# Perceiver stream: where GpSimd's key subtractions and the context loads stand, and how the short last key chunks are grouped

## Chip, cores and metric

The kernel runs on one core of a Trainium2 chip. Its time is the device time of one execution in microseconds (us), as the median of three runs. TensorE (PE), VectorE (DVE), ScalarE (ACT), GpSimd (POOL) and SyncE (SP) each run their own instructions in program order. Here all DMAs are issued from SyncE's queue, which is in order too.

## What is computed

Two perceiver layers on 32 batches of 64 queries of width 256. Only the two cross attentions touch the large input, a context of 1601 keys per batch:

```python
x = x + _L0_xattn_ref(_layernorm(x), ctx_1024, ctx_1024, wq, bq, wk, bk, wv, bv, wo, bo)
x = x + _L0_attn_ref(_layernorm(x), ...)        # self attention
x = x + _L0_ffn_ref(_layernorm(x), ...)         # attention over the best half of the tokens
x = x + _L1_xattn_ref(_layernorm(x), ctx_1024, mask, q_w, q_b, k_w, k_b, v_w, v_b)
x = x + _L1_attn_ref(...); x = x + _L1_ffn_ref(...)
# a cross attention, 16 heads of 16:
scores = softmax(einsum('bhqd,bhkd->bhqk', qh, kh)); attn = einsum('bhqk,bhkd->bhqd', scores, vh)
```

## The kernel before, in words

The method `stream` does both cross attentions and, between them in time, the first layer's self attention and feed-forward. It counts 64 batches: 32 of the first layer, then the same 32 of the second. What follows it (the second layer's self attention and feed-forward, from about 3400 us on) is not touched.

**Units.** A unit `u` is one batch and 4 of its 16 heads: 256 units, each of 4 iterations `i`. In an iteration TensorE gets, in this order: score products `sp` for the next unit's row maxima (`maxima`, L1093; 3, 3, 2 and 0 groups in iterations 0 to 3, VectorE reduces each, L1098; three PSUM buffers), the value products `acc` of the iteration before (`weighted`, L1145), score products `tp` for the exponentials (`probabilities`, L1128, evacuated by ScalarE as `e`, L1133), a step of the other attentions (`group_step`), and key and value products (`keys_values`).

**Keys and values.** The 1601 keys of a batch are 13 chunks of 128; the last holds 65 keys, or 72 with padding. A key group is two chunks, `KEYGROUPS`: six full groups and a seventh with the short chunk alone. A group goes through these steps, written as generators:

- `load` (L892): a DMA of the context into `raw`, three buffers.
- `split`: VectorE rounds `raw` to `chi` (L904), GpSimd subtracts, `clo` (L905).
- `keys`: 12 f32r matmuls into the bank `kp` (L980), ScalarE adds the bias, `kr` (L986).
- `parted`: VectorE casts `kr` to bf16 (L936), GpSimd subtracts (`kr`, L937), VectorE casts the rest, GpSimd subtracts again (`ks`, L937), and SyncE stores the three parts to DRAM, `kd` (L942). Each `yield` of it ends a step; `tick` runs one step of each open group.
- `values`: 12 matmuls, or 6 for the short chunk, into the bank `vp` (L1006); ScalarE copies them to `v` (L1011).

`projections` puts these in order: a load four groups ahead just before `keys(i)`, the split two groups ahead just before `values(i)`. `keys_values` runs banks until the work made, in the planner's column counts (`PER_BATCH`), meets a target that lies 1.8 batches ahead of the unit.

**Fetches.** At a unit's start `fetch` calls `tick` and then issues the seven DMAs (L1065, L1069) that bring the keys of the unit after next from `kd` into `kst`, three buffers; the buffer comes free with the last `tp` of the unit before. `tick` is called again in each iteration just ahead of `probabilities`, so there are five ticks in a unit. In the tick, the cast and the subtraction behind it stand together:

```python
                    nc.vector.tensor_copy(ks[:, s, :, :m], x)
                    eng.tensor_tensor(
                        x if s == 0 else ks[:, 2, :, :m], x, ks[:, s, :, :m], ALU.subtract
                    )
                    if s or not quick:
                        yield
```

Of the kernel before, what the change touches and what calls it, by code (L numbers as in the profile page):

```python
# [19 lines left out]
F32 = mybir.dt.float32  # L20
# [9 lines left out]
P = 128  # L30
# [7 lines left out]
NKE = 1608  # L38
KEYGROUPS = [(c, min(2, NCH - c)) for c in range(0, NCH, 2)]
GB = len(KEYGROUPS)  # L40
KG = 2 * P
NATGROUPS = [(0, 401), (401, 400), (801, 400), (1201, 400)]
# [17 lines left out]
class Kernel:  # L60
# [411 lines left out]
    def stream(self):  # L472
        nc, tc, ins = self.nc, self.tc, self.ins
        with ExitStack() as ctx:
# [13 lines left out]
            dkv = pool("dk", 3, space=DRAM)  # L488
# [399 lines left out]
            def load(b, g, raw=None):  # L888
                c0, n = KEYGROUPS[g]
                if raw is None:  # L890
                    raw = inp.tile([P, 2, KG], F32, tag="raw", name=f"raw{b}_{g}", bufs=3)
                nc.sync.dma_start(  # L892
                    raw[:, :, : n * P],
                    ins["ctx_1024"][b % NB, :, c0 * P : (c0 + n) * P].rearrange(
                        "(c p) n -> p c n", p=P
                    ),
                )
                return raw

            def split(b, g, raw):  # L900
                n = KEYGROUPS[g][1] * P
                hi = inp.tile([P, 2, KG], F32R, tag="chi", name=f"chi{b}_{g}", bufs=3)
                lo = inp.tile([P, 2, KG], F32R, tag="clo", name=f"clo{b}_{g}", bufs=3)
                nc.vector.tensor_copy(hi[:, :, :n], raw[:, :, :n])  # L904
                (nc.vector if b == 0 and g < 2 else nc.gpsimd).tensor_tensor(  # L905
                    lo[:, :, :n], raw[:, :, :n], hi[:, :, :n].bitcast(F32), ALU.subtract
                )
                return hi, lo

            kds, vs, ksts, cuts = {}, {}, {}, []  # L910

            vring = []
            for g, (_, n) in enumerate(KEYGROUPS):
                vring.append([
                    vp_.tile([P, n, 16, 17], F32, tag=f"v{g}_{r}", name=f"v{g}_{r}")
                    for r in range(3 if g < 5 else 2)
                ])
                for v in vring[g]:
                    nc.gpsimd.memset(v[:, :, :, 16:17], 1.0)

            def tick(b=-1):

                for one in list(cuts):
                    while next(one[1], True) is None:
                        if one[0] > b:
                            break
                    else:
                        cuts.remove(one)

            def parted(b, g, k0, m, r, quick):  # L930

                ks = work.tile([P, 3, 2, KG], BF16, tag="ks", name=f"ks{b}_{g}")
                eng = nc.vector if quick else nc.gpsimd
                x = r[:, :, :m]
                for s in range(2):
                    nc.vector.tensor_copy(ks[:, s, :, :m], x)  # L936
                    eng.tensor_tensor(  # L937
                        x if s == 0 else ks[:, 2, :, :m], x, ks[:, s, :, :m], ALU.subtract
                    )
                    if s or not quick:  # L940
                        yield
                nc.sync.dma_start(  # L942
                    kds[b][:, :, k0 : k0 + m].rearrange("s (c p) n -> p s c n", p=P),
                    ks[:, :, :, :m],
                )

            seq = [(b, g) for b in range(2 * NB) for g in range(len(KEYGROUPS))]

# [9 lines left out]
            keyed, valued = [0], [0]  # L958

            def projections():  # L960


                parts = {0: split(*seq[0], raws.pop(0))}
                wk, wv = cut(wraw.pop(), 0, 1), None
                turn = NB * GB

                def keys(i):
                    b, g = seq[i]
                    c0, n = KEYGROUPS[g]
                    m = min(n * P, NKE - c0 * P)  # L970
                    hi, lo = parts[i]
                    if g == 0:
                        kds[b] = dkv.tile([3, D, NKP], BF16, tag="kd", name=f"kd{b}")
                    r = work.tile([P, 2, KG], F32, tag="kr", name=f"kr{b}_{g}")
                    kp = bank(f"kp{b}_{g}").rearrange("p (c n) -> p c n", c=2)
                    for oc in range(2):
                        j = 0
                        for w, x in ((0, hi), (1, hi), (0, lo)):
                            for cc in range(2):
                                nc.tensor.matmul(  # L980
                                    kp[:, oc, :m], wk[w][:, cc, oc * P : (oc + 1) * P],
                                    x[:, cc, :m], start=(j == 0), stop=(j == 5),
                                )
                                j += 1
                    for oc in range(2):
                        nc.scalar.activation(  # L986
                            r[:, oc, :m], kp[:, oc, :m], AF.Identity,
                            bias=self.bk[layer(b)][:, oc : oc + 1],
                        )
                    cuts.append((b, parted(b, g, c0 * P, m, r, i < 10)))  # L990
                    keyed[0] = i + 1
                    return 12 * max(m, P)

                def values(i):
                    b, g = seq[i]
                    n = KEYGROUPS[g][1]
                    hi, lo = parts.pop(i)
                    v = vring[g][b % len(vring[g])]
                    vs.setdefault(b, []).extend(v[:, i0] for i0 in range(n))
                    vp = bank(f"vp{b}_{g}").rearrange("p (i d) -> p i d", i=2)  # L1000
                    for i1 in range(n):
                        o = slice(i1 * P, (i1 + 1) * P)
                        j = 0
                        for cc in range(2):
                            for x, w in ((hi, 0), (hi, 1), (lo, 0)):
                                nc.tensor.matmul(  # L1006
                                    vp[:, i1, :], x[:, cc, o], wv[w][:, cc, :],
                                    start=(j == 0), stop=(j == 5),
                                )
                                j += 1  # L1010
                    nc.scalar.copy(  # L1011
                        v[:, :, :, :16],
                        vp[:, :n, :].rearrange("p c (h d) -> p c h d", d=16),
                    )
                    valued[0] = i + 1
                    return 6 * n * D

                def fetched(i):
                    if i < len(seq) and i not in raws and i not in parts:
                        raws[i] = load(*seq[i])  # L1020

                parts[1] = split(*seq[1], raws.pop(1))
                two = []
                for i in range(len(seq)):
                    if i == turn - 2:
                        two.append(weight(1, 1))
                    elif i == turn - 1:
                        two.append(weight(1, 2))
                    elif i > 4 and i != turn:
                        fetched(i + 4)  # L1030
                    yield keys(i)
                    if i + 2 < len(seq):
                        parts[i + 2] = split(*seq[i + 2], raws.pop(i + 2))
# [4 lines left out]
                    if i == turn - 1:  # L1038
                        wk = cut(two[0], 1, 1)
                        fetched(i + 3)  # L1040
                        fetched(i + 4)
                    if i == turn:
                        wv = cut(two[1], 1, 2)
                        fetched(i + 4)
                    yield values(i)

            PER_BATCH = sum(
                12 * max(min(n * P, NKE - c0 * P), P) + 6 * D * n for c0, n in KEYGROUPS
            )
# [6 lines left out]
            def fetch(u):  # L1056

                b, q4 = divmod(u, 4)
                while keyed[0] < (b + 1) * GB:
                    made[0] += next(proj)  # L1060
                tick(b)
# [74 lines left out]
            def weighted(u, i, e):  # L1136
# [3 lines left out]
                v = vs[b]  # L1140
                assert valued[0] > b * GB + i
                for c in range(2 * i, min(2 * i + 2, NCH)):
                    m = min(P, NK - c * P)
                    for h in range(4):
                        nc.tensor.matmul(  # L1145
                            acc[32 * h : 32 * h + 17, slot, :], v[c][:m, 4 * q4 + h, :],
# [52 lines left out]
            raws = {0: load(*seq[0])}  # L1199
            wraw = [weight(0, 1)]  # L1200
            self.bk = self.biases(wp, 0, "k")
            raws[1] = load(*seq[1])
# [5 lines left out]
            raws[2] = load(*seq[2])  # L1208
            early = kp_.tile([P, 4, NKE], BF16, tag="kst", name="early")
            early = early.rearrange("p h n -> p (h n)").bitcast(F32)  # L1210
            for i in range(5):
                raws[3 + i] = load(
                    *seq[3 + i],
# [9 lines left out]
            def banks_made(n):  # L1223
                for _ in range(n):
                    made[0] += next(proj)
                    tick()
# [4 lines left out]
            while keyed[0] < GB:  # L1231
# [16 lines left out]
            for u in range(NU):  # L1248
# [11 lines left out]
                for i in range(4):  # L1260
# [10 lines left out]
                    tick()  # L1271
# [5 lines left out]
                    keys_values(LEAD + (4 * u + i + 1) / 16.0, 0.15)  # L1277
                    end_step()
# [925 lines left out]
```

## Time and profile before

| | |
|---|---|
| three runs | 3994.56 us median (3990.45 to 4006.71) |
| the profiled execution | 3997.09 us, of which its span 3995.4 |
| instructions | 155308 |
| DMA | 647 MB, 162 GB/s over the span |
| `kd<-ks` stores | 384 of 384 KB, 64 of 108 KB |
| `raw` loads | 380 of 256 KB, 63 of 128 KB |
| `kst<-kd` fetches | 1536 of 201 KB |

A page's group line names line, engine and operation, the tile written and those read, partitions x elements and type, and the count; then busy time in us and the mean in ns of one; then the engine's idle time just before, and who ended it. Two groups of each engine that the change touches:

```profile
L937 POOL TENSOR_TENSOR kr<-kr,ks 128x512 f32<-128x512 f32 x438 | 487.5, 1113 | 1148.3 <-DVE ks L936 1083.8
L936 DVE CAST ks<-kr 128x512 bf16<-128x512 f32 (+1 forms) x896 | 537.5, 600 | 527.3 <-ACT kr L986 279.7
...
L905 POOL TENSOR_TENSOR clo<-raw,chi 128x512 fp32r<-128x512 f32 x441 | 541.3, 1227 | 78.5 <-issue 16.8
```

The first line reads: 438 subtractions of 1113 ns; GpSimd was idle for 1148 us before them, 1084 of these until VectorE's cast was done. Rows that keep shapes apart give the 128x512 casts (768) 608 ns, the 128x144 casts (128) 551, `chi` casts of 128x512 (380) 505, and the short group's evacuations by ScalarE 318.

### The profile page before, as it was taken

The numbers are of one execution on the slowest core, as the hardware profiler recorded it, in microseconds if no ns is written. First come the engines' busy times: TensorE is split into PE (matmuls) and PEld (weight loads), VectorE is DVE, ScalarE is ACT, GpSimd is POOL, SyncE is SP. The second block draws the span as 40 slices with busy tenths as digits, with TensorE's granted clock in tenths as the row PEclk, the third lists the DMA queues.
The fourth block names the chain that finished last, engine by engine and source line by source line (L and its number), as shares of the span: only waits on it lengthen the run. The fifth ranks groups of instructions, "written<-read, shape, count | busy, mean of one in ns | idle before, by whom it ended". The sixth has DMA issues, their size and how long they took to land.

```text
span 3995.4 us, 155308 instructions
## 1 busy us (share of the span) xinstructions
PE 3594.5 (90%) x66703; PEld 2893.7 (72%) x66703; DVE 2785.4 (70%) x6723; ACT 2016.5 (50%) x4015; POOL 2007.6 (50%) x2234
## 2 busy tenths in 40 slices
PE   6899999999999998999999999998999998674589
PEld 6788878778788887777777777777777776331467
DVE  5567767666767766667776766666766665688879
ACT  2455555555555554455555555554555554142453
POOL 3455555555555555555655556555555552004246
PEclk8999999999999999999999999999999999785689
DMA  6888768767777776767777777667787786100000
GB/s 171 217 210 205 196 160 203 190 175 193 187 188 196 191 183 174 198 171 190 178 185 183 183 188 193 176 166 187 196 205 197 198 202 165 55 1 1 1 4 20
DMA packets 669952, 647.05 MB, mean 162 GB/s; under 512 B 98064, under 2 KB 567376, under 8 KB 669136
## 3 DMA queue, kind: packets, MB, share of 16 engines
q1 hardware_dynamic: 669264, 637.12, 62.8%
q8 instruction: 524, 8.59, 1.0%
q14 instruction: 164, 1.34, 0.1%
HBM read 465.97 MB, written 170.98 MB: 159 GB/s over the span
## 4 chain that ended last, share of the span: by engine, by line
PE 59%; DVE 18%; DMA 7%; issue 5%; POOL 5%; SPq 3%; ACT 2%; POOLq 0%; ACTq 0%; DVEq 0%
PE kp L980 14%; PE vp L1006 11%; PE tp L1128 9%; PE sp L1093 8%; PE acc L1145 7%; DVE mx L1098 3%; DMA kst<-kd 3%; DVE ks L936 3%; SPq L1065 3%; DMA raw<-in_ctx_dram 2%; DMA kd<-ks 2%; POOL kr L937 1%; DVE sa_mxq L1463 1%; ACT kr L986 1%; DVE chi L904 1%
## 5 line engine op out<-in xcount | busy, mean ns | idle before, releaser
L1098 DVE TENSOR_REDUCE mx<-sp 128x1 f32<-128x400 f32 (+1 forms) x2048 | 1048.8, 565 | 368.1 <-PE sp L1093 366.5
L1133 ACT ACTIVATE e<-tp 128x512 f32<-128x512 f32 (+1 forms) x1792 | 932.8, 565 | 699.0 <-PE tp L1128 692.5
L937 POOL TENSOR_TENSOR kr<-kr,ks 128x512 f32<-128x512 f32 x438 | 487.5, 1113 | 1148.3 <-DVE ks L936 1083.8
L936 DVE CAST ks<-kr 128x512 bf16<-128x512 f32 (+1 forms) x896 | 537.5, 600 | 527.3 <-ACT kr L986 279.7
L1093 PE MATMUL sp<-kst,xa_qst 96*32 96x400 bf16 (+3 forms) x8192 | 529.0, 346 | 161.5 <-DVE mx L1098 63.0
L986 ACT ACTIVATE kr<-kp,bk 128x256 f32<-128x256 f32 (+1 forms) x896 | 356.7, 449 | 462.9 <-PE kp L980 434.5
L1128 PE MATMUL tp<-xa_qst,kst 98*128 98x64 bf16 (+2 forms) x13312 | 585.4, 196 | 0.8 <-issue 0.7
L1145 PE MATMUL acc<-e,v 128*17 128x64 f32 x26624 | 574.0, 222 | 9.0 <-ACT e L1133 6.1
L905 POOL TENSOR_TENSOR clo<-raw,chi 128x512 fp32r<-128x512 f32 x441 | 541.3, 1227 | 78.5 <-issue 16.8
L1145 PEld LDWEIGHTS acc<-e,v 128*17 128x17 f32 x26624 | 468.3, 99 | 151.4 <-ACT e L1133 23.2
L937 POOL TENSOR_TENSOR ks<-kr,ks 128x512 bf16<-128x512 f32 x438 | 478.7, 1093 | 184.7 <-DVE ks L936 177.0
L1128 PEld LDWEIGHTS <-kst 98*128 98x128 bf16 (+2 forms) x13312 | 464.9, 100 | 113.7 <-issue 6.9
L1006 PE MATMUL vp<-w_hi,chi 128*128 128x256 f32 x1664 | 517.6, 311 | 10.8 <-DVE w_hi L205 10.8
L1006 PE MATMUL vp<-w_lo,chi 128*128 128x256 f32 x1664 | 476.0, 286 | 2.1 <-DVE w_lo L206 2.1
L1006 PE MATMUL vp<-w_hi,clo 128*128 128x256 f32 x1664 | 474.3, 285 | 0.0
L1011 ACT COPY v<-vp 128x512 f32<-128x512 f32 (+1 forms) x448 | 249.9, 558 | 335.2 <-PE vp L1006 333.8
L980 PE MATMUL kp<-chi,w_hi 128*128 128x256 f32 (+1 forms) x1792 | 402.8, 307 | 6.8 <-DVE w_hi L205 5.4
L1093 PEld LDWEIGHTS <-xa_qst 96*32 96x32 bf16 (+1 forms) x8192 | 163.0, 95 | 337.9 <-issue 196.1
L980 PE MATMUL kp<-chi,w_lo 128*128 128x256 f32 (+1 forms) x1792 | 365.8, 287 | 1.6 <-DVE w_lo L206 1.2
L980 PE MATMUL kp<-clo,w_hi 128*128 128x256 f32 (+1 forms) x1792 | 363.4, 285 | 2.7 <-POOL clo L905 2.7
L1006 PEld LDWEIGHTS vp<-w_hi,chi 128*128 128x128 f32 x1664 | 322.3, 194 | 43.9 <-ACT e L1133 18.6
L1006 PEld LDWEIGHTS vp<-w_lo,chi 128*128 128x128 f32 x1664 | 322.6, 194 | 3.2 <-DVE w_lo L206 2.7
(734 smaller groups left out, 5183.3 us busy)
## 6 DMA issues: line engine op xcount, KB each, us to landing
kst<-kd SPq DMA_DIRECT2D x1536, 201.0 KB
kd<-ks SPq DMA_DIRECT2D x384, 384.0 KB
raw<-in_ctx_dram SPq DMA_DIRECT2D x380, 256.0 KB
xa_qst<-xa_qd SPq DMA_DIRECT2D x96, 128.0 KB
raw<-in_ctx_dram SPq DMA_DIRECT2D x63, 128.0 KB
kd<-ks SPq DMA_DIRECT2D x64, 108.0 KB
xa_qd<-xa_qs SPq DMA_DIRECT2D x16, 384.0 KB
kst<-rows SPq DMA_DIRECT2D x128, 37.7 KB
```

The costliest lines, as they stand in the source:

```text
L905: (nc.vector if b == 0 and g < 2 else nc.gpsimd).tensor_tensor(lo[:, :, :n], raw[:, :, :n], hi[:, :, :n].bitcast(F32), ALU.subtract)
L936: nc.vector.tensor_copy(ks[:, s, :, :m], x)
L937: eng.tensor_tensor(x if s == 0 else ks[:, 2, :, :m], x, ks[:, s, :, :m], ALU.subtract)
L980: nc.tensor.matmul(kp[:, oc, :m], wk[w][:, cc, oc * P : (oc + 1) * P], x[:, cc, :m], start=(j == 0), stop=(j == 5),)
L986: nc.scalar.activation(r[:, oc, :m], kp[:, oc, :m], AF.Identity, bias=self.bk[layer(b)][:, oc : oc + 1],)
L1006: nc.tensor.matmul(vp[:, i1, :], x[:, cc, o], wv[w][:, cc, :], start=(j == 0), stop=(j == 5),)
L1011: nc.scalar.copy(v[:, :, :, :16], vp[:, :n, :].rearrange("p c (h d) -> p c h d", d=16),)
L1093: nc.tensor.matmul(sp[32 * w : 32 * w + 32, :n], q[:NR, h0 + 2 * p + w // 2, t0 : t0 + 32], k[:NR, 2 * p + w // 2, k0 : k0 + n], start=Tru ...
L1098: nc.vector.tensor_reduce(mx[:, p, g : g + 1], sp[:, :n], AX.X, ALU.max)
L1128: nc.tensor.matmul(sp[:m, c, h, :], k[:NA, h, k0 : k0 + m], q[:NA, h0 + h, tok], start=True, stop=True,)
L1133: nc.scalar.activation(e[:m, :two], sp[:m, :two], AF.Exp)
L1145: nc.tensor.matmul(acc[32 * h : 32 * h + 17, slot, :], v[c][:m, 4 * q4 + h, :], e[:m, c - 2 * i, h, :], start=(c == 0), stop=(c == NCH - 1),)
```

## The change

Three things change.

1. The short last chunks of batches b and b + 1 (b even) form one group: `seq` now lists pairs of chunks, 6.5 groups a batch, 416 in all instead of 448. `width` is 72 for such a group. It takes two loads and two stores, 12 key matmuls of 144 columns, and 12 value matmuls with 72 columns of weights. It is made after the six full groups of the even batch, so a fourth `kd` buffer is added.
2. The steps of `parted` carry a kind, "first" or "last". Casts and stores are "first" and run at the old places of `tick`; GpSimd's subtractions are "last" and run at a new call of `tick` at the end of the iteration's program, behind `keys_values`, where the split's `clo` stands.
3. A load is no longer issued ahead of `keys`. It is put on a list just after the split two groups ahead, and issued at the next "first" tick, after that tick's stores and, in a fetch, ahead of the fetch's DMAs.

```diff
-KEYGROUPS = [(c, min(2, NCH - c)) for c in range(0, NCH, 2)]
+MLAST = NKE - (NCH - 1) * P
-            dkv = pool("dk", 3, space=DRAM)
+            dkv = pool("dk", 4, space=DRAM)
+            seq = []
+            for b in range(2 * NB):
+                seq += [((b, c), (b, c + 1)) for c in range(0, NCH - 1, 2)]
+                if b % 2 == 0:
+                    seq.append(((b, NCH - 1), (b + 1, NCH - 1)))
+            def width(i):
+                return P if seq[i][0][0] == seq[i][1][0] else MLAST
-            def tick(b=-1):
+            def tick(kind, b=-1):
                 for one in list(cuts):
-                    while next(one[1], True) is None:
+                    while one[1] == kind or one[0] <= b:
+                        one[1] = next(one[2], None)
+                        if one[1] is None:
+                            cuts.remove(one)
+                            break
                         if one[0] > b:
                             break
-                    else:
-                        cuts.remove(one)
+                while kind == "first" and wanted:
+                    i = wanted.pop(0)
+                    raws[i] = load(i)
                 for s in range(2):
+                    if not (s and quick):
+                        yield "first"
                     nc.vector.tensor_copy(ks[:, s, :, :m], x)
+                    if not quick:
+                        yield "last"
                     eng.tensor_tensor(
                         x if s == 0 else ks[:, 2, :, :m], x, ks[:, s, :, :m], ALU.subtract
                     )
-                    if s or not quick:
-                        yield
+                yield "first"
-                    elif i > 4 and i != turn:
-                        fetched(i + 4)
                     yield keys(i)
                     if i + 2 < len(seq):
-                        parts[i + 2] = split(*seq[i + 2], raws.pop(i + 2))
+                        parts[i + 2] = split(i + 2)
+                    elif i > 3 and i != turn - 2:
+                        fetched(i + 4)
                     yield values(i)
-                    tick()
+                    tick("first")
...
                     keys_values(LEAD + (4 * u + i + 1) / 16.0, 0.15)
+                    tick("last")
                     end_step()
```

In the changed `fetched` the load is appended to `wanted` instead of being issued.

## The prediction

> **What bounds the kernel now.** I read the page first, then the busy time by stretch, TensorE's timeline, the waits of TensorE and of SyncE's queue, and one stall in the timeline. The page gives busy shares and, by fortieth of the span, TensorE's busy tenths, its granted clock and the DMA share:
>
> ```profile
> PE 3594.5 (90%) x66703; PEld 2893.7 (72%) x66703; DVE 2785.4 (70%) x6723; ACT 2016.5 (50%) x4015; POOL 2007.6 (50%) x2234
> ...
> PE   6899999999999998999999999998999998674589
> ...
> PEclk8999999999999999999999999999999999785689
> DMA  6888768767777776767777777667787786100000
> ```
>
> The stream, which alone the change touches, fills the first 34 slices. From 100 to 3345 us TensorE is busy 3071 of 3245 us, VectorE 2221, GpSimd 1780, ScalarE 1736. TensorE sets the pace. Its durations overlap, so I cost a matmul by the distance of its start to the next. TensorE's timeline, start and length first:
>
> ```profile
> 462.71 1.03 PE L798 MATMUL ff_z<-wg,ff_xT 128*128 128x1 f32 x8
> ...
> 1500.09 0.40 PE L980 MATMUL kp<-chi,w_hi 128*128 128x256 f32 x2
> 1500.33 0.40 PE L980 MATMUL kp<-chi,w_lo 128*128 128x256 f32 x2
> ...
> 1505.26 0.39 PE L980 MATMUL kp<-chi,w_hi 128*128 128x72 f32 x2
> 1505.48 0.39 PE L980 MATMUL kp<-chi,w_lo 128*128 128x72 f32 x2
> ```
>
> Two matmuls of 256 columns take 0.24 us, 0.12 each; two of the short chunk's 72 columns 0.22, 0.112 each. Eight of ONE column, with 128x128 f32 weights too, take (1.03 - 0.25) / 7 = 0.111 each. So a short chunk's matmul pays for its weights, and its columns are free.
>
> Second, TensorE's waits from 100 to 3345 us, then SyncE's over the span (total us, times, longest):
>
> ```profile
> PE sp L1093 <- DVE mx L1098: 61.4, 35, 10.2
> PE sp L1093 <- DMA kst<-kd: 29.6, 14, 6.2
> PE sp L1093 <- DMA raw<-in_ctx_dram: 15.7, 15, 2.3
> ```
> ```profile
> SPq L892 <- POOL clo L905: 671.6, 209, 10.1
> SPq L942 <- POOL ks L937: 608.0, 243, 16.8
> ```
>
> TensorE's idle time is before the score matmuls: half for VectorE's maxima, half for a `kst` fetch (where another DMA is named, the fetch was last too: in nearly all these places its last packet lands 0.5 to 1.7 us before the start). SyncE's one queue stands a third of the span behind GpSimd. One such stall:
>
> ```profile
> 2140.64 1.28 POOL L937 TENSOR_TENSOR ks<-kr,ks 128x512 bf16<-128x512 f32 x1 [0.64 <-DVE ks L936]
> ...
> 2140.99 1.21 DVE L936 CAST ks<-kr 128x512 bf16<-128x512 f32 x1
> ...
> 2141.94 0.37 SPq L942 DMA_DIRECT2D kd<-ks  x1
> ...
> 2142.41 6.22 SPq L1065 DMA_DIRECT2D kst<-kd  x6
> ...
> 2144.54 1.48 DVE L936 CAST ks<-kr 128x512 bf16<-128x512 f32 x1 [1.04 <-POOL kr L937]
> 2145.08 0.70 PE L1093 MATMUL sp<-kst,xa_qst 97*32 97x401 bf16 x12 [2.63 <-DMA kst<-kd]
> ```
>
> GpSimd's second subtraction ends at 2141.92, the store waits for it, the fetch stands behind the store, TensorE loses 2.63 us. VectorE's casts last 1.21 and 1.48 us where the undisturbed ones last 0.42: they overlap a GpSimd operation and end with it.
>
> **Part 1, short chunks paired.** 64 short key products of 12 matmuls become 32 of 12 with 144 columns; value matmuls stay 12 per pair. Removed: 384 x 0.112 = 43 us. No row shows 144 columns of this type. Upper bound: [...]0.24 us, which loses 6 us instead of gaining 43; but then 72 columns would need 0.12, and they take 0.112. Lower bound: the weights' 0.112, nearest to the rows (1, 72, 256 columns: 0.111, 0.112, 0.12); I take it. A rule speaks against it: the Trainium skill, "TensorE: Matmul & The Clock Gate", section "The mechanism", has a weight load overlap a running matmul only where row groups differ. Loads of 0.112 plus columns at 0.42 ns (512 bf16 columns start 0.215 us apart) would then give 0.142 (72) and 0.172 (144), a gain of 24 x 0.142 - 12 x 0.172 = 1.34 us a pair, the same 43 us; the 256-column row (0.12, not 0.22) refutes the overlap half anyway.
> There are also 64 fewer banks of matmuls. Around one, starts lie 0.03 (last `tp` to first) and 0.21 us (last to next `sp`) apart, against 0.127 from `tp` straight to `sp`: 0.11 more; its first matmul takes 0.2 instead of 0.12. 64 x 0.19 = 12 us. **Together 55 us of TensorE**, which is the path.
> ScalarE, VectorE and GpSimd lose 64 to 128 short instructions each (evacuation 0.32, cast 0.55, subtractions 0.55 and 0.47 us): beside TensorE, counted as nothing. Loads and stores stay 448 each; the short loads shrink.
>
> **Part 2, subtractions last.** GpSimd's order in an iteration turns from `kr` subtraction, `clo` to `clo`, `kr` subtraction; the `ks` subtraction comes one iteration later in both. Removed: long casts. Mean 0.608 against 0.43 (768), 0.551 against 0.24 (128), `chi` 0.505 against 0.42 (380): 137 + 40 + 32 = 209 us of VectorE. After the change GpSimd's work starts behind the last cast and runs beside maxima, which last 0.566 us at the median and 0.575 at the 90th percentile.
> Added: the second cast now waits for `clo` (1.27 us) and then the subtraction (1.17). By the program's order 54% of the items have no maximum between the two casts (last two iterations of a unit): 416 x 0.54 x 1.27 = 285 us of VectorE's waiting. Queued behind that cast are the next unit's maxima, for which TensorE waits. The cover: from a unit's last `sp` to the fourth `sp` of the next (three buffers) TensorE has two `acc` (0.62 each), two `tp` (0.64), three banks (1.65), three `sp` (0.63) and small ones, some 8.5 us; VectorE in that time has three casts, `chi`, 2.5 us of waiting, neg/mm and three maxima, 6.3 us. It holds with 2 us to spare, less where self-attention's steps join. Bounds for the 61 us of maxima waits: -61 to +90 (a third of the 285 uncovered); I take -10.
>
> **Part 3, loads one tick later, and what stands before a fetch.** A load now goes out 4 to 6 ticks (five a unit of 13 us) before its split, not 6 to 8. Loads land 3.9 us after issue (99%: 6.4) and then lie 14 us (1%: 7.6) before `chi` reads them; two ticks (5.2 us) less leaves 8.8 (1%: 2.4). No cost taken, bound +10. SyncE no longer stands for `clo` (671 us), but the store's 608 us stay, and SyncE's idling itself isn't on the path; the fetch behind it is. By the program's order a store is issued right before the fetch's DMAs in 74% of the fetches now, in 37% after. The trace of before has both kinds: 179 fetches with such a store go out 2.8 us (median) after their buffer is free, and TensorE loses 54 us behind them, 0.30 each; the 60 without go out 0.15 us after it and cost 7.5 us, 0.125 each. So 184 x 0.30 + 65 x 0.125 = 63 us becomes 91 x 0.30 + 158 x 0.125 = 47: **-16 us**. For even batches the last store moves up to the unit just before its fetch, one or two iterations ahead; it lands in 2.6 us: nothing, bound +30 (32 x 1 us).
>
> **The clock.** A stall costs more than itself (windows view; the number before "DMA share" is the granted clock):
>
> ```profile
> 2142.40:2145.10 2.70, 0.07 (x5) 0.11 (x6) 1.66 (x2) 0.59 (x1) 2.70 (x3) 1.00 1.10 221
> 2145.10:2150.00 4.90, 4.90 (x100) 3.60 (x100) 3.81 (x7) 1.55 (x3) 1.79 (x2) 0.65 1.01 263
> ```
>
> After 2.6 us idle the clock is 0.65 for 4.9 us: 1.7 us lost. The same page's section "What's actually happening" has the clock halve after an idle window of about 3.4 us; by that, stalls this short cost only themselves. In this trace nearly all of the 33 half-clock stretches of the stream (160 us) lie at a stall of 0.8 us or more. By the rule parts 2 and 3 bring 26 us; by the rows about as much again, half the saved stalls being long enough: I add 9.
>
> **Sum**, against the profiled execution, 3997.1 us (span 3995.4 and 1.7 around it; 0.06% above the median 3994.6): 55 + 10 + 16 + 9 = 90. For the median: **3905 us**. The stages after 3400 us stay.
>
> **Rivals.**
> A. The stalls only change place (VectorE's freed time goes into waiting for GpSimd), TensorE's work still shrinks: 3995 - 55 = 3940. For it: long waits on maxima also come from GpSimd's chains of small operations. Chance 0.2.
> B. Slower: the second cast, behind `clo`, holds the next unit's maxima. 285 us of waiting; it decides from one fifth (55 us) reaching TensorE. At one third, 95 - 55 = +40: 4035. For it: 35 waits on maxima already show that the cover is sometimes gone. Against it: the 209 us of long casts go. Chance 0.11.
> C. 144 columns cost 0.24 us, the pairing saves only banks: 3995 - 12 + 6 - 35 = 3954. Chance 0.04.
> D. Fetch and maxima stalls mostly vanish: 55 + 100 and more, below 3850. Chance 0.07.
> The forecast: 0.58.
>
> **Numbers.** The range takes the forecast with its bounds, A and most of C, and leaves out B and D: 3855 to 3965. About 0.5% (20 us) is what a measurement of this kernel can tell from no change. Faster than 3975: 0.56 of the forecast's 0.58, 0.18 of A's 0.2, C and D: 0.85. Within: the rest of the forecast and of A, 0.02 of B: 0.06. Slower: B's other 0.09.
>
> **What would show it.** Key matmuls of 144 columns starting 0.112 us apart (0.24: part 1 is wrong); casts' means near 0.45; SyncE's wait for `clo` near nothing; TensorE's waits on fetches down by a quarter or more; waits of `ks` on `kr` above today's 190 us with waits on maxima not above 61. Maxima waits above 120 us would make the forecast wrong (B), as would `chi` waiting for its load.

## The result, and the profile after

The changed kernel takes 4149.56 us (median of 4 runs, 4147.04 to 4156.55) against 3996.65 of the kernel before, measured beside it: a ratio of 1.0383, 95% interval 1.0357 to 1.0408. It is 3.8% slower; 3905 was forecast. The profiled execution has a span of 4148.0 us against 3995.4. The last `tp` of the stream ends at 3565.8 us instead of 3409.8: 156 us, so the whole loss lies in the stream.

The page of the changed kernel, busy time and slices:

```profile
PE 3634.9 (88%) x66319; PEld 2897.2 (70%) x66319; DVE 2615.5 (63%) x6627; ACT 2005.0 (48%) x3919; POOL 1932.0 (47%) x2138
...
PE   7899989999899998989999989999888898585578
PEclk9899999999999998999998999999999999795689
DMA  6887757666666776677776677767777777200000
```

VectorE, GpSimd and ScalarE all do less than before, and 384 matmuls are gone; TensorE is busy for more microseconds because more of them are granted half the clock. Over the stream (100 to 3490 us) the mean granted clock is 0.95, against 0.98 before (100 to 3345). No engine became full: the time went into waiting. First VectorE's waits in the stream (100 to 3490 us), then TensorE's, then SyncE's over the span (total us, times, longest):

```profile
DVE ks L965 <- POOL kr L968: 616.1, 282, 13.3
DVE mx L1124 <- PE sp L1119: 313.8, 202, 4.4
DVE ks L965 <- ACT kr L1016: 224.2, 159, 5.0
```
```profile
PE sp L1119 <- DVE mx L1124: 130.5, 80, 10.6
PE sp L1119 <- DMA kst<-kd: 25.7, 14, 4.4
PE rp L1133 <- DVE mm L1129: 24.8, 24, 9.5
```
```profile
SPq L973 <- POOL ks L968: 1295.8, 276, 16.6
```

Before (100 to 3345 us), the first line of VectorE read

```profile
DVE ks L936 <- POOL kr L937: 188.3, 173, 11.3
```

Both the number of waits (+109) and their mean (1.1 to 2.2 us) have grown. TensorE's waits on maxima went from 61.4 to 130.5 us, and waits of the row products `rp` on `mm`, the result of the maxima, from 0.4 to 24.8. Taken together, 84 of TensorE's 106 waits of these two kinds (145 of 157 us, up to the last `tp`) have a wait of VectorE for `kr` in them or within the 3 us ahead of them. SyncE's wait for `clo`, 672 us before, is down to 1.6; the stores' wait for GpSimd has doubled, while TensorE's waits on fetches hardly moved (29.6 to 25.7).

One such wait in the changed kernel's timeline:

```profile
2244.66 1.40 DVE L921 CAST chi<-raw 128x512 fp32r<-128x512 f32 x1
...
2245.73 1.34 POOL L968 TENSOR_TENSOR ks<-kr,ks 128x512 bf16<-128x512 f32 x1
...
2247.03 1.27 POOL L922 TENSOR_TENSOR clo<-raw,chi 128x512 fp32r<-128x512 f32 x1
...
2248.25 1.16 POOL L968 TENSOR_TENSOR kr<-kr,ks 128x512 f32<-128x512 f32 x1
...
2249.44 0.43 DVE L965 CAST ks<-kr 128x512 bf16<-128x512 f32 x1 [3.38 <-POOL kr L968]
2249.79 1.53 DVE L1124 TENSOR_REDUCE mx<-sp 128x1 f32<-128x401 f32 x3
...
2250.41 1.01 PE L1119 MATMUL sp<-kst,xa_qst 97*32 97x400 bf16 x8 [3.31 <-DVE mx L1124]
```

Read it from below: TensorE stands 3.31 us for maxima, which stand behind VectorE's second cast, which waits for GpSimd's `kr`, which now stands behind `clo`. Here `clo` itself begins a microsecond after its `chi` is done (2246.06), because another item's `ks` is ahead of it on GpSimd. The more frequent case is shorter: in 241 of the 284 waits of a cast on `kr` (474 of 618 us, over the whole span) `clo` begins 0.13 us after the end of `chi`, which VectorE makes at the end of its iteration. VectorE, through with `chi`, comes to the cast and stands there until GpSimd has done `clo` and the subtraction. What a stall of TensorE costs beyond itself stands in the windows view (the number before the DMA share is the granted clock):

```profile
2246.10:2250.40 4.30, 0.99 (x32) 0.80 (x25) 0.96 (x3) 1.39 (x3) 3.76 (x4) 0.86 0.54 149
2250.40:2257.00 6.60, 6.59 (x112) 5.25 (x111) 2.71 (x6) 1.69 (x4) 0.70 (x1) 0.57 1.00 247
```

After the stall TensorE runs 6.6 us at 0.57 of its clock.

To see where the time is, I added up from each trace the distance from every matmul's start to the next, from the first `tp` (at about 79 us) to the last: gaps in which TensorE is idle, and the rest by whether the full or half the clock was granted. "Work" counts half-clock time at half, and the other half as lost; that is a little too much loss, as value matmuls start 0.213 us apart at half clock against 0.12 (in the column of the subtractions alone, where no work was taken away, the sum shows 24 us less).

| us | before | pairing alone | subtractions alone | changed | changed, second cast moved | best version |
|---|---|---|---|---|---|---|
| idle gaps | 190.9 | 207.0 | 294.5 | 305.9 | 201.1 | 160.7 |
| lost in half clock | 78.2 | 97.4 | 166.7 | 167.7 | 79.2 | 58.8 |
| work | 3061.3 | 3026.1 | 3036.9 | 3012.7 | 3010.6 | 3009.8 |

From before to changed: 115 us more gaps, 89 us more in half clock, 49 us less work. The other columns are kernels of the next section.

### The profile page after: what moved, and what is told of

It is laid out like the page before. It is cut to its first block, busy times and chain, and to the rows that moved or that the text cites. A ratio compares the mean times of both kernels' runs of the same rounds, so it can differ in the third digit from the quotient of the medians.

```text
span 4148.0 us, 153826 instructions
## 1 busy us (share of the span) xinstructions
PE 3634.9 (88%) x66319; PEld 2897.2 (70%) x66319; DVE 2615.5 (63%) x6627; ACT 2005.0 (48%) x3919; POOL 1932.0 (47%) x2138
## 5 line engine op out<-in xcount | busy, mean ns | idle before, releaser
L922 POOL TENSOR_TENSOR clo<-raw,chi 128x512 fp32r<-128x512 f32 (+1 forms) x409 | 508.2, 1243 | 1233.0 <-issue 267.6
L965 DVE CAST ks<-kr 128x512 bf16<-128x512 f32 (+1 forms) x832 | 403.1, 485 | 895.5 <-POOL kr L968 618.4
L1119 PE MATMUL sp<-kst,xa_qst 96*32 96x400 bf16 (+3 forms) x8192 | 559.9, 354 | 235.1 <-DVE mx L1124 132.3
L968 POOL TENSOR_TENSOR ks<-kr,ks 128x512 bf16<-128x512 f32 (+1 forms) x406 | 465.4, 1146 | 249.5 <-DVE ks L965 226.6
L1038 PE MATMUL vp<-w_hi,chi 128*128 128x256 f32 (+1 forms) x1664 | 511.1, 307 | 13.2 <-DVE w_hi L204 10.2
L1038 PE MATMUL vp<-w_lo,chi 128*128 128x256 f32 (+1 forms) x1664 | 473.6, 285 | 2.1 <-DVE w_lo L205 2.1
L1038 PE MATMUL vp<-w_hi,clo 128*128 128x256 f32 (+1 forms) x1664 | 472.8, 284 | 0.0
L968 POOL TENSOR_TENSOR kr<-kr,ks 128x512 f32<-128x512 f32 (+1 forms) x406 | 459.0, 1131 | 11.4 <-DVE ks L965 11.0
L1038 PEld LDWEIGHTS vp<-w_hi,chi 128*128 128x128 f32 (+1 forms) x1664 | 314.4, 189 | 39.8 <-ACT e L1159 19.5
L1038 PEld LDWEIGHTS vp<-w_lo,chi 128*128 128x128 f32 (+1 forms) x1664 | 314.5, 189 | 4.9 <-DVE w_lo L205 2.7
```

What stands on the lines that cost most here:

```text
L922: (nc.vector if i < 2 else nc.gpsimd).tensor_tensor(lo[:, :, :n], raw[:, :, :n], hi[:, :, :n].bitcast(F32), ALU.subtract)
L968: eng.tensor_tensor(x if s == 0 else ks[:, 2, :, :m], x, ks[:, s, :, :m], ALU.subtract)
L1038: nc.tensor.matmul(vp[:w_, i1, :], x[:, cc, o], wv[w][:, cc, :], start=(j == 0), stop=(j == 5),)
L1119: nc.tensor.matmul(sp[32 * w : 32 * w + 32, :n], q[:NR, h0 + 2 * p + w // 2, t0 : t0 + 32], k[:NR, 2 * p + w // 2, k0 : k0 + n], start=Tru ...
```

## Experiments

All ratios are against the kernel before, measured on the same chip.

### The parts alone

My theory after the result: the first subtraction, now behind `clo`, holds VectorE's second cast and so the maxima. Rivals: the pairing makes the banks lumpy; late loads or late stores disturb SyncE. The first kernel takes the subtractions back:

```diff
-                    if not quick:
-                        yield "last"
```

> The changed kernel with both of GpSimd's key subtractions back in the tick, right behind their cast; short chunks still paired, loads still one tick later. Theory (the subtraction behind clo holds the second cast, and through it VectorE's maxima): the wait of ks on GpSimd's kr falls from 618 us to about 190, the pairing's 55 us and some of the fetch stalls show, 3905 to 3945 us. Rival 1 (pairing makes the banks lumpy, one 144-column group per two batches): stays above 4050. Rival 2 (late loads or late stores disturb SyncE's queue): stays above 4050, with waits on DMAs grown.

Measured 3995.56 us, ratio 0.9996 (0.9983 to 1.0009). The loss is gone, so it lies in the subtractions; but the 55 us of the pairing aren't there either, which neither the theory nor a rival had said.

The second takes the loads back too (`fetched(i + 4)` ahead of `yield keys(i)`, issued at once):

> Pairing alone: subtractions in the tick, loads issued ahead of keys(i) as before the change. Theory: 3996 - 55 = about 3940 us, stalls and maxima waits as before (63 us). Rival 1 (the pairing is what costs): above 4050 us. The difference to the kernel with late loads as well is the worth of the late loads: 16 us by the prediction's step, 0 to +30 if they come too late.

Measured 3995.74 us, 1.0002 (0.9988 to 1.0016). Pairing alone gives nothing, and nothing differs between late and early loads. The third puts the subtractions alone into the kernel before, with the two kinds of `tick`:

> The kernel before with the subtractions alone moved behind keys_values; no pairing, loads early. Theory: +155 of the whole change and +55 that the pairing hid, about 4200 us, with the wait of ks on GpSimd's kr above 600 us and waits of sp on maxima near 130. Rivals 1 and 2 (pairing or loads cost): within 40 us of 3996.

Measured 4160.06 us, 1.0412 (1.0389 to 1.0434), with the wait of `ks` on `kr` at 637.9 us in the stream. The subtractions alone lose 163 us, more than the whole change. The fourth puts the late loads alone into the kernel before:

> The kernel before with the loads alone one tick later. Theory and prediction: SyncE no longer waits for clo (672 us to near 0), fetches go out sooner, -16 us: 3980. Rival 2 (a late load holds chi, and so TensorE): 4010 or more, with chi waiting for the load's DMA.

Measured 3997.22 us, 1.0002 (0.9987 to 1.0016). The loads' wait for `clo` on SyncE fell to 24.8 us (from 671.6), and the stores' wait for `ks` rose to 1186.9 us (from 608.0): the stall only moved down its queue. TensorE's waits of `sp` on DMAs of any name went from 76 to 71 us in the stream.

### Which subtraction, and why behind

Two kernels leave only one of the subtractions late:

```diff
-                    if not quick:
+                    if not quick and s == 1:
                         yield "last"
```

> The changed kernel with only GpSimd's second subtraction (ks) at the end of the iteration's program; the first (kr), for which VectorE's second cast waits, back right behind its cast. Theory (what costs is the second cast held behind clo): the wait of ks on GpSimd's kr near 190 us, time near the 3996 us that pairing and late loads gave without any subtraction last; at most +20 for later stores. Rival 2 (the subtraction that comes late delays the store, and so SyncE and the fetch): near 4150 us, with waits on kst well above today's. Rival 4 (any GpSimd work put beside VectorE's maxima costs): about half of the 154 us, 4070.

Measured 3987.4 us, 0.9975 (0.9961 to 0.9989): no loss, even 11 us gained.

> The changed kernel with only the first subtraction (kr) at the end of the iteration's program, the second right behind its cast. Theory: the whole loss, 4130 to 4170 us, wait of ks on kr near 600 us. Rival 2: near 4000. Rival 4: about 4070.

With `s == 0` instead: 4135.19 us, 1.0354 (1.0321 to 1.0386). The loss, but for 14 us that lie within the intervals, hangs on the first subtraction, the one that VectorE's second cast waits for. The late one that only a store waits for is no cost, though SyncE waits 1053 us for it. The next kernel keeps both late but ahead of `clo`:

```diff
-                    keys_values(LEAD + (4 * u + i + 1) / 16.0, 0.15)
                     tick("last")
+                    keys_values(LEAD + (4 * u + i + 1) / 16.0, 0.15)
```

> The changed kernel with the late tick moved ahead of keys_values, so that both subtractions stay late but stand ahead of clo on GpSimd. Theory: the cast no longer waits for clo's 1.27 us and for what clo waits for; wait of ks on kr 190 to 250 us, time 3990 to 4030. If being behind the group step's GpSimd work or beside the maxima is what costs (rival 4): above 4080.

Measured 4030.57 us, 1.0086 (1.0054 to 1.0117); waits of `ks` on `kr` 220.9 us in the stream. So 119 us of the 154 come from standing behind `keys_values`, of whose operations GpSimd runs `clo` alone; some 35 (to 3996) remain with both late and ahead of `clo`.

Then a tick more between the first subtraction and the second cast:

```diff
+                    if s and not quick:
+                        yield "first"
```

> The changed kernel with one more tick between the first subtraction and the second cast, so that VectorE meets the cast one tick later; all subtractions stay at the end of the program, behind clo. Theory: most of the 618 us of VectorE's waiting goes, and with it most of the loss, 3990 to 4060; stores go out one tick later, which by rival 2 makes it worse than 4150. Rival 4: unchanged, near 4150.

Measured 4090.76 us, 1.0231 (1.0186 to 1.0277): 59 us came back, less than the 90 and more that I expected. Waits on `kr` were halved (313.0 us), but items held `ks` longer, and casts now waited for the store of the buffer:

```profile
DVE ks L967 <- POOL kr L970: 313.0, 153, 9.4
DVE ks L967 <- DMA kd<-ks: 233.2, 83, 7.1
```

That leaves it open whether the place of the wait matters or its length. The next pair answers it.

### Moving the waiter

The second cast gets a kind of its own, run only in iterations 0, 1 and 2, where three, three and two maxima of the next unit stand ahead of the tick. It isn't run in a fetch's tick or in iteration 3, behind which the next unit's maxima come. Stores get a kind too, so that each is issued a tick after its subtraction as before. On the changed kernel, subtractions still behind `clo`:

```diff
-                        yield "first"
+                        yield "second" if s else "first"
...
-                yield "first"
+                yield "store"
...
+                    tick("store")
+                    if i < 3:
+                        tick("second")
                     tick("first")
                     late = [
```

> The changed kernel with VectorE's second cast run only in the ticks of iterations 0, 1 and 2, each of which stands behind three maxima; both subtractions stay late and behind clo. Theory (VectorE waits at a place where the next unit's maxima come next): waits of ks on GpSimd's kr fall below 200 us and most of the 154 us comes back, 3990 to 4050. If it is that keys arrive later (stores one or two ticks later here) or that GpSimd works at another time: 4150 or more.

Measured 3958.8 us, 0.9904 (0.9885 to 0.9924): 191 us below the changed kernel, more than its whole loss. Both subtractions still stand behind `clo`, and second casts are run later, none earlier. In this kernel's stream, TensorE's waits and VectorE's:

```profile
PE rp L1134 <- DVE mm L1130: 51.1, 43, 10.6
...
PE sp L1120 <- DVE mx L1125: 11.8, 17, 2.4
```
```profile
DVE ks L965 <- POOL kr L968: 228.5, 136, 11.8
DVE ks L965 <- DMA kd<-ks: 111.7, 35, 8.8
```

VectorE still waits 340 us for `kr` and for buffers together, more than before the change (227); but `sp` waits 12 us on maxima instead of 130. The rest shows up at `rp`, which needs the last maxima of a unit: 63 us with `sp`, against 155 in the changed kernel and 62 before. This kernel alone can't say how much came from the wait's new place and how much from the cast itself, which left the old place too. The comparison that can is with the last kernel of these experiments, which has the second cast here and no late subtraction (3941.39 us):

```profile
DVE ks L965 <- DMA kd<-ks: 103.3, 24, 7.2
...
DVE ks L965 <- POOL kr L966: 26.7, 12, 8.7
```

At the new place, making both subtractions late adds 210 us to these waits (130 to 340) and costs 17 us. At the old place it adds 421 (216 in the first kernel of the experiments, 637 in the changed one) and costs 154. A microsecond of VectorE's waiting costs 0.08 us at the one place and 0.37 at the other: what cost was above all where VectorE waited.

The same move on the kernel before:

> The kernel before with the second cast only behind maxima, nothing else. Theory: its 190 us of VectorE's waits for kr fall, maxima waits (61 us) with them: 3960 to 3990. If covered: 3997.

Measured 3967.5 us, 0.9922 (0.9906 to 0.9939). 30 us came back, with VectorE's waits for `kr` down from 188 to 30 us and those for buffers up from 38 to 169; here the waits and the cast's own time at the old place aren't separated. And on the version with only the second subtraction late:

> The changed kernel with the first subtraction back behind its cast, only the second late, and the second cast only behind maxima. Theory: the remaining 195 us of VectorE's waits for kr go too, 3950 to 3985 us. If these waits are covered already: 3987; if the later stores cost: above 4000.

Measured 3897.55 us, 0.9748 (0.9729 to 0.9766), 2.5% faster than before and below what I expected: the best version. TensorE's and VectorE's waits in its stream:

```profile
PE sp L1120 <- DVE mx L1125: 35.1, 40, 8.6
...
PE sp L1120 <- DMA kst<-kd: 14.9, 7, 4.5
```
```profile
DVE ks L965 <- DMA kd<-ks: 167.7, 54, 8.9
...
DVE ks L965 <- POOL kr L968: 28.4, 14, 8.8
```

VectorE's wait for `kr` is nearly gone, and TensorE's waits on maxima and fetches are about half of before's.

Whether the 11 us of the late second subtraction is its own was asked of the kernel before, with that alone:

> The kernel before with only the second subtraction at the end of the iteration's program; no pairing, loads early. If the 10 us is that subtraction's own: 3986 us. If it came from the late loads together with it (SyncE's loads no longer wait): 3997.

Measured 3983.82 us, 0.9963 (0.9951 to 0.9975): it is.

### Where the pairing's 55 us went

In pairing alone, the trace gives 41 us less of key products' work (633.4 to 592.1, half clock at half), near the 43 forecast. But it gives 16 us more gaps and 19 more in half clock. Counting what stands between a `tp` and the next `sp` or `acc` (a bank is the key or the value products of one group): iterations without a bank ahead of score products rose from 142 to 191, and the stalls behind them from 53.0 to 105.4 us; those without a bank where `acc` comes next, from 11 to 43, 6.1 to 20.5 us; stalls behind iterations with a bank fell from 104 to 58. My idea: TensorE, without a bank to do, runs into the maxima. So I moved the empty iterations to iteration 2, behind which no score products come:

```diff
-                    keys_values(LEAD + (4 * u + i + 1) / 16.0, 0.15)
+                    t = LEAD + (4 * u + i + 1) / 16.0
+                    skip = i == 2 and u % 4 != 3 and made[0] > (t - 0.15) * PER_BATCH
...
+                        made[0] += next(proj, 0)
+                    if not skip:
+                        keys_values(t - 0.15, 0.05)
```

> Pairing alone (subtractions and loads as before the change), with the planner changed so that the iterations without a bank lie where no score group for the maxima follows (iteration 2 of three units in four); each other iteration makes one bank. Theory (the pairing's 55 us went into stalls of score products that follow an iteration without a bank: 191 such places with 105 us of stalls, against 142 with 53 before): those stalls fall below 30 us, about 90 us lost instead at 190 value products that wait for exponentials (0.5 each), and less half clock behind; 3950 to 3985 us. Rival (TensorE's work isn't the bound at all): 3996 as pairing alone.

Measured 4012.4 us, 1.0031 (1.0018 to 1.0044): worse. Waits of `sp` on maxima did fall, to 11.7 us, but the products next in line now wait, `acc` for exponentials and `rp` for the maxima's result:

```profile
PE acc L1169 <- ACT e L1159: 62.6, 126, 0.8
PE rp L1133 <- DVE mm L1129: 30.2, 18, 12.8
```

The unpaired control:

> The kernel before, unpaired, with the same change of the planner (iteration 2 of every second unit goes without a bank). It is the control for the run with pairing: theory, 3970 to 4000 us, and the pairing worth 20 to 50 us between the two. If the pairing is worth nothing here either, the short chunks' TensorE time isn't what was saved.

Measured 4020.09 us, 1.0051 (1.0035 to 1.0067): pairing is worth some 8 us here, if anything, since the two intervals overlap. And with only the second subtraction late:

> The changed kernel with only the second subtraction late (3987 us) and the even placement of banks: theory, the gains add, 3940 to 3980 us; rival, 3987 as without the even placement.

Measured 4130.05 us, 1.0331 (1.0304 to 1.0358), a miss by 150. There SyncE's stores wait 372.6 us for `ks` casts beside 960.1 for subtractions, and `sp` waits over 140 us on DMAs. Why this placement makes the late subtraction so costly was not tried.

A test of the premise that TensorE sets the pace:

> Pairing alone, with the third product of every key bank (clo with the high weights, 4 of 12 matmuls) left out, so the keys are less precise: 1664 x 0.12 = 200 us of TensorE work gone from the same banks in the same places. If TensorE's work sets the pace, as the prediction has it: 3796 us. If it is the loop of score products, maxima and casts: only a part comes back, 3880 to 3950, with TensorE's gaps grown by the rest.

Measured 3903.4 us, 0.9749 (0.9721 to 0.9778): of 200 us of TensorE's work about 95 came back. By the trace, against pairing alone, gaps grew from 207.0 to 271.4 us and half clock took 32 more. TensorE's time is paid out at half here. Where the rest is held, the waits of `sp` say in part: those on maxima grew by 18 us (88.5 to 106.5), those on `kst` fetches by 22 (11.1 to 33.2). So TensorE runs into the maxima and into the fetches alike.

If that is so, the pairing should pay once the stalls are gone. Unpaired, loads early, second subtraction late, second cast moved:

> The kernel before with the second subtraction late and the second cast only behind maxima; unpaired, loads early. If the pairing's TensorE time is paid out once the stalls are gone: 3935 to 3955 us, 40 to 55 above the paired 3898. If the pairing is worth nothing here either: 3898.

Measured 3988.38 us, 0.9973 (0.9960 to 0.9986).

> Pairing and late loads with the second cast only behind maxima, no subtraction late. Unpaired this was 3967.5 us. If the pairing pays here: 3910 to 3930 us, and the late second subtraction accounts for the other 15 to 30 of the way to 3898. If it doesn't pay: 3967.

Measured 3941.39 us, 0.9849 (0.9829 to 0.9868). With the second cast moved, pairing and late loads together are worth 26 us (3967.5 to 3941.4) without a late subtraction and 91 (3988.4 to 3897.6) with the late second one, where they were worth nothing on the old place. Both of these times lie outside what was expected. 91 is more than the pairing's work. By the same sums as in the table above, with the late second subtraction 46 us of work, 22 of gaps and 28 of half clock go; without it 52 us of work go, but 22 of gaps and 7 of half clock come. So in the first case the work is paid out and stalls go as well; whether the pairing or the late loads took the stalls away was not separated. The late second subtraction gains 44 us with them and loses 21 without; why it loses there is open.

## Why the prediction was wrong, step by step

- **Part 1, size right, payment wrong.** 144 columns start 0.112 us apart (median of 330 at full clock; a paired bank in the changed kernel's timeline, two matmuls a line, 0.22 us):

```profile
1150.54 0.39 PE L1010 MATMUL kp<-clo,w_hi 128*128 128x144 f32 x2
1150.77 0.39 PE L1010 MATMUL kp<-chi,w_hi 128*128 128x144 f32 x2
1150.99 0.39 PE L1010 MATMUL kp<-chi,w_lo 128*128 128x144 f32 x2
```

  The 43 us were 41. The 12 us for fewer banks don't show in the sum: with pairing alone TensorE's work fell by 35 us in all, and the distances from `tp`, `sp` and `acc` to what follows them grew by 24 us together. And "55 us of TensorE, which is the path" was wrong in its second half: the path goes through the maxima as well, and where a bank is missing, cover for them is missing (the counts in the section above).
- **Part 2, the step that failed.** "It holds with 2 us to spare", and "I take -10". By the runs this term alone is +163 us, outside its bounds of -61 to +90. The mechanism was on paper, as rival B, with the right place and a price of 285 us of VectorE's waiting, of which I let a third reach TensorE at most. The waiting measured 428 us more (188.3 to 616.1). Two counts were wrong. First, the wait: I charged `clo`'s 1.27 us on top. But `clo` and the subtraction begin only when VectorE's `chi` is done (241 waits of 284), or behind another operation of GpSimd (41): the mean wait is 2.2 us. Second, the cover: 8.5 us of TensorE's work assumed three banks in the time. The 832 banks in 1024 iterations make it 2.4 on average, which leaves an average unit about 1 us to spare by the same sum, and they are not evenly spread: in the changed kernel 234 of 1024 iterations have none, and 172 of the 279 us of stalls ahead of `sp`, `acc` and `rp` follow these. The units that stall aren't average. The half clock nearly doubled it (115 us of gaps, 89 of clock), which the forecast knew for gains and didn't apply to this loss.
- **Long casts.** The forecast took 209 us off VectorE. Casts of 128x512 went from 608 to 488 ns (92 us), `chi` from 505 to 454 (19), the short ones from 70 to 29 us in all, half of them gone: 153. They did not fall to the undisturbed 0.42 us (the two long ones shown in the prediction end 0.28 and 0.29 us after GpSimd's operation, not with it), and no run shows a gain from the time that was freed.
- **Part 3.** "No cost taken" was right, -16 was not: nothing, whether alone on the kernel before or on top of the pairing. The store behind GpSimd takes over the wait. Rows that show a fetch behind a store being late don't show that the store, put elsewhere, lets the fetch be early.
- **The clock.** The row against the rule of the Trainium skill ("TensorE: Matmul & The Clock Gate", "What's actually happening", an idle window of some 3.4 us): the row was right. In the trace of before a stall of 1.28 us is followed, 1.6 us later, by a stretch at half the clock (windows view: stall, what follows, and the stretch):

```profile
1859.84:1861.12 1.28, 0.00 (x1) 0.03 (x2) 1.28 (x2) 0.53 (x2) 0.99 (x1) 1.00 1.14 346
1861.12:1862.70 1.58, 1.58 (x39) 1.32 (x40) 1.51 (x5) 0.33 (x1) 1.16 (x1) 1.00 0.96 304
1862.70:1866.11 3.41, 3.41 (x36) 2.66 (x38) 2.42 (x10) 1.59 (x4) 1.35 (x5) 0.50 0.34 103
```

  The 3.31 us stall of the changed kernel is followed by 0.57, and half-clock losses rise and fall with gaps in every column of the table.
- **Rivals.** B happened and had 0.11; its number, 4035, was too low by the same two counts. A's thought, that stalls change place while TensorE's work shrinks, is what the pairing did, but with nothing left over.
- **What would show it.** The mark set for B (waits on maxima above 120 us) appeared, 130.5. Of the forecast's own marks, TensorE's waits on fetches fell by an eighth (29.6 to 25.7) instead of a quarter.

## What to carry to other kernels

Before an operation is moved back in an in-order queue, find who waits for it and what stands behind that waiter in its own program: here the same two late subtractions cost 154 us where the waiting cast stood ahead of the next maxima, and 17 where it stood behind some. Moving the waiter gained 54 us with both subtractions in their old place (3995.6 to 3941.4), and together with the late second one it gave the best version. A saving on the busiest engine need not be paid out where other waits end at the same place: here 200 us less work gave 95, and 41 us less gave nothing. Cover has to be checked at the places that stall, not for the average unit.

## What was not expected of the hardware

Matmuls of 128x128 f32 weights start 0.111 us apart with 1 column, 0.112 with 72 and with 144, and 0.12 with 256. In the stream half clock comes in stretches of 3.41 us or whole multiples of it. In several places of the trace of before they follow stalls of 1.3 to 1.6 us. One (at 2508 us) follows 3.4 us in which TensorE never stood idle, but spent 2.2 us on products over 32 partitions (`sa_kp`, `sa_v`); whether these are the cause is open. What half clock adds differs: 78 us to 191 us of gaps before, and 89 more to the 115 us of gaps that the change added.
